# Summing two states per step on GpSimd or on TensorE: moving the switch from step 190 to step 224

## The chip, the cores and the metric

The kernel runs on one core of a Trainium2 chip. A core has five engines with a queue each: TensorE (PE in the profile; PEld is its weight load), VectorE (DVE), ScalarE (ACT), GpSimd (POOL) and SyncE (SP, which issues most of the DMAs). Each engine works through its own queue in order and waits at semaphores for the others. The metric is the device time of one execution in microseconds (us); several executions are timed, and the median is given. One further execution is profiled, and all views of the profile come from that one.

## The reference, cut to what matters

The input x has 2 sequences of 2048 tokens with 256 features. After a layer norm it goes two ways. One is a Mamba block followed by an MLP; the other is a mixture of 8 experts with the 2 best chosen per token. The result is x + s * silu(g), with s from the first way and g from the second. The core of the Mamba block, and the part that the change touches, is the recurrence over time with 512 channels and 16 states per channel:

```python
def step(h, ts):
    dt_t, B_t, C_t, u_t = ts
    dA = jnp.exp(dt_t[..., None] * A)
    h = h * dA + (dt_t * u_t)[..., None] * B_t[:, None, :]
    y = jnp.einsum('bds,bs->bd', h, C_t)
    return (h, y)
```

followed by `y = ys + xc * D`, `y = y * silu(z)`, the output projection, `x = x + ...` and `x = x + silu(rmsnorm(x) @ mlp_w1.T) @ mlp_w2.T`. The einsum sums h * C over the 16 states. Everything is computed in float32.

## The kernel before

**Tiling.** The 4096 tokens are cut into 8 blocks of 512 (`c`, 0 to 7; blocks 0 to 3 are the first sequence, 4 to 7 the second). The 512 channels are 4 groups of 128 partitions (`d`). The 16 states are taken in pairs (`g`, 0 to 7). A **step** `n` is one block, one channel group and one pair of states: `n = 32 c + 8 d + g`, 256 steps in all. Steps 190 and 191 are the last two of block 5, steps 192 to 223 are block 6, steps 224 to 255 are block 7.

**One step** runs over several engines:

- ACT computes the two decays `da` (`exps`, L1387), two steps ahead.
- DVE multiplies dt*u by the broadcast B of both states (L1498, into PSUM) and runs two scans along time, one per state (L1502), which give `h`.
- POOL saves the last column of `h` for the next block (`save`, L1424; not in blocks 3 and 7), multiplies `h` by the broadcast C (`times_c`, L1430, one instruction of 128x1024) and, if the step is *paired*, adds the two states into one (L1432, 128x512).
- PE adds the step to the sum over the states in PSUM by multiplying `h` with an identity matrix (`accumulate`, L1400): one product for a paired step, two for an unpaired one. It does so three steps later (`LAG = 3`). The first product of a group is the skip `xc * D` (L1396).

`h` has five buffers, so the scan of a step waits until PE has read the step five before it. The tiles B and C are loaded once per block for each `g` by SP (`load_bc`, L762), as soon as the old ones were read for the last time: B by DVE's L1498, C by POOL's L1430.

**Work between the steps.** The function `draw` lets other work in between by a budget of PE time per half step (`HALF = 1.93`): the projections of the next block (`front`: PE L621, ACT L631 to L638, DVE L646, ACT L660, PE L666, PE L685, then dt with POOL's L700, L712 and L713), the gate z (`gate_z`, PE L772), the output projection (`out_proj`, PE L821, DVE L855) and the FFN tiles: first 39 tiles of the experts, then the MLP in 16 half blocks of 256 tokens. `Later` puts off the instructions that follow on other engines by a number of half steps. The budget does not look at whether a step is paired, so the written order of the other instructions is independent of it.

**A half block of the MLP** takes: rows from DRAM, scaled on ACT (L1119), turned on PE (L934), first product on PE (L946), silu on ACT (L1144, with a table load, L183, before and after), second product on PE (L958). Beside it, POOL issues four gathers of the two experts' rows (L1185), ACT weighs them (L1199), POOL adds them (L1203), ACT takes a tanh (L1207), and DVE ends the half: L1218, L1228 (needs the tanh), L1229, L1230, then SP stores it. The rows are gathered into tiles that the half before has used, so the gathers follow its L1229. The PSUM tile of the second product shares its one bank with the output projection (L821), which therefore follows L1230. The first products, the turned rows and the projections share three banks, in order (`bank("h", ...)`).

Which steps are paired is said by one line:

```python
return n >= 8 and not (n >= 190 and n % 2 == 0) and n < NS - 1
```

Here `NS` is 256. Before step 8 no step is paired, from 8 to 189 every step, and from 190 on only the odd ones.

Of the kernel before, what the change touches and what calls it, by code (L numbers as in the profile page):

```python
# [52 lines left out]
def kernel(  # L53
# [1321 lines left out]
    NS = NBLK * ND * (DS // 2)  # L1375
# [15 lines left out]
    def accumulate(n):  # L1391
        c, d, g = at[n]
        if g == 0:
            y_n[c, d] = ring("y", 1)
            ys[c, d] = ps_1.tile([P, T], F32, tag="y", name=f"y{c}_{d}")
            nc.tensor.matmul(ys[c, d], ddiag[:, d, :], xcs[c, d], start=True, stop=False)  # L1396
            skips[0] += 1
        nq = 1 if paired(n) else 2
        for q in range(nq):
            nc.tensor.matmul(  # L1400
                ys[c, d], ident, hts[n][:, q, :], start=False,
                stop=(g == DS // 2 - 1 and q == nq - 1),
            )
        if g == DS // 2 - 1:
            y, sz, twice = ys[c, d], szs[c, d], 1.0 if d else 0.5

            def gated():
                nc.vector.scalar_tensor_tensor(sz, y, twice, sz, ALU.mult, ALU.mult)
                y_made.add((c, d))

            later.put(gated, y_n[c, d], after=2)
# [14 lines left out]
    def times_c(n):  # L1426
        c, d, g = at[n]

        engine = nc.vector if n == NS - 1 else nc.gpsimd
        engine.tensor_tensor(hts[n], hts[n], bct[c, "C", g], ALU.mult)  # L1430
        if paired(n):
            nc.gpsimd.tensor_tensor(hts[n][:, 0, :], hts[n][:, 0, :], hts[n][:, 1, :], ALU.add)  # L1432

    def paired(n):

        return n >= 8 and not (n >= 190 and n % 2 == 0) and n < NS - 1

    def draw(share):

# [146 lines left out]
```

## Time and profile before

| what | value |
|---|---|
| time, median of 3 runs | 1489.96 us (1489.83 to 1492.37) |
| profiled execution, its own time | 1505.4 us |
| its span (first to last instruction) | 1503.7 us |
| POOL L1430 (times C), per instruction | 2371 ns mean, 255 instructions |
| POOL L1432 (adds two states) | 1287 ns mean, 214 instructions |
| PE L1400 (identity product), trace records | 596; one product leaves two records |
| DVE L1502 (scan) | 1270 ns mean |
| start of L1430 for steps 190, 222, 224 | 1083.66, 1278.36, 1286.08 us |

The page gives times from one profiled execution, which took some 15 us longer than the median of the timed runs. In a group's row, after the count, stand the busy time in us and the mean of one in ns, then the engine's idle time before these instructions and what ended most of it. In a list of waits, `A <- B: 15.7, 5, 6.2` says that A sat idle for 15.7 us in all until B ended, 5 times, at longest 6.2. In a timeline a row has the start and the length in us, and in brackets the idle time before it. "issue" is a wait that the profile ties to nothing.

### The profile page before, as it was taken

Reading aid. Unit: us, or ns where it says so; the run is one execution under the profiler, and the core shown is the slowest. Engines: PE = TensorE matmul, PEld = TensorE weight load, DVE = VectorE, ACT = ScalarE, POOL = GpSimd, SP = SyncE. Lnnn points to the kernel's source line nnn. Section 1 sums busy time; section 2 is a strip of 40 time slices with the busy share of each in tenths; the row PEclk is TensorE's granted clock in tenths of the full one; section 3 lists DMA queues with packets and bytes.
Section 4 is the critical chain, followed back from the end, with each engine's and each line's share of the span. In section 5 each row is a group of like instructions: output and inputs, shape, how many; then the busy total and the mean of one; then the engine's idle time right before and its main releaser. Section 6 shows DMA issues by size and latency. Waiting matters only on the chain.

```text
span 1503.7 us, 18025 instructions
## 1 busy us (share of the span) xinstructions
PE 1347.4 (90%) x5122; PEld 944.1 (63%) x5122; DVE 1217.2 (81%) x1351; ACT 978.5 (65%) x1765; POOL 1188.3 (79%) x964
## 2 busy tenths in 40 slices
PE   5744799999999999999999999979878998999958
PEld 4531467765776677766776677546655666667726
DVE  7448888889798998799888988999767967888853
ACT  4742777458655776568656865677648988778932
POOL 2665779987898799968997899889975888777860
PEclk9556899999999999999999999999999999999989
DMA  5568134962477345924492449445830116412110
GB/s 187 198 234 304 46 99 145 306 220 76 125 230 280 92 131 180 335 95 121 158 363 74 129 140 331 167 139 175 268 114 8 55 53 211 139 53 60 57 57 14
DMA packets 169317, 231.85 MB, mean 154 GB/s; under 512 B 19825, under 2 KB 139761, under 8 KB 169217
## 3 DMA queue, kind: packets, MB, share of 16 engines
q1 hardware_dynamic: 163072, 213.91, 42.9%
q0 software_dynamic: 6144, 16.79, 3.4%
q8 instruction: 41, 0.67, 0.2%
q14 instruction: 60, 0.48, 0.1%
HBM read 195.12 MB, written 35.52 MB: 153 GB/s over the span
## 4 chain that ended last, share of the span: by engine, by line
PE 44%; POOL 25%; DVE 10%; ACT 10%; issue 6%; DMA 4%; another core or an unknown queue 1%; POOLq 0%; DVEq 0%; SPq 0%; ACTq 0%
POOL h L1430 13%; PE phe L946 9%; PE y L1400 8%; PE poe L958 8%; POOL h L1432 6%; PE pom L958 4%; PE phm L946 4%; PE po L821 3%; ACT L183 2%; PE px L621 2%; DVE h L1502 2%; DMA B<-bcd 2%; ACT da L1387 2%; PE pz L772 2%; DMA C<-bcd 1%
## 5 line engine op out<-in xcount | busy, mean ns | idle before, releaser
L1430 POOL TENSOR_TENSOR h<-h,C 128x1024 f32<-128x1024 f32 x255 | 604.1, 2371 | 36.7 <-issue 11.5
L1502 DVE TENSOR_TENSOR_SCAN h<-da,hs,b 128x512 f32<-128x512 f32 x384 | 477.6, 1270 | 41.4 <-PE y L1400 10.8
L1387 ACT ACTIVATE da<-dt,a_neg 128x512 f32<-128x512 f32 x512 | 352.8, 717 | 93.3 <-DVE h L1502 87.2
L1400 PE MATMUL y<-h,ident 128*128 128x512 f32 x596 | 307.3, 617 | 34.6 <-POOL h L1432 17.5
L1498 DVE TENSOR_TENSOR b<-du,B 128x1024 f32<-128x1024 f32 x256 | 315.0, 1231 | 18.4 <-DMA B<-bcd 9.1
L1432 POOL TENSOR_TENSOR h<-h 128x512 f32<-128x512 f32 x214 | 275.4, 1287 | 16.8
L946 PE MATMUL phe<-xsTe,w_e 128*128 128x256 f32 (+1 forms) x1248 | 268.1, 366 | 9.4 <-ACT xsTe L937 7.6
L946 PEld LDWEIGHTS phe<-xsTe,w_e 128*128 128x128 f32 x1248 | 225.4, 194 | 72.7 <-issue 27.6
L958 PE MATMUL poe<-w_e,hide 128*128 128x256 f32 x1136 | 265.2, 380 | 2.5 <-ACT hide L1053 2.5
L958 PEld LDWEIGHTS poe<-w_e,hide 128*128 128x128 f32 x1136 | 213.8, 190 | 65.1 <-issue 33.5
L1053 ACT ACTIVATE hide<-phe,b 128x256 f32<-128x256 f32 (+1 forms) x312 | 123.6, 450 | 140.8 <-PE phe L946 140.4
L1400 PEld LDWEIGHTS y<-h,ident 128*128 128x128 f32 x596 | 112.2, 197 | 124.0 <-issue 60.5
L1502 DVE TENSOR_TENSOR_SCAN h<-da,b 128x512 f32<-128x512 f32 x128 | 151.3, 1210 | 12.7 <-PE y L1400 4.8
L183 ACT ACT_TABLE_LOAD x121 | 155.2, 1283 | 2.9 <-PEq L1573 0.8
L946 PE MATMUL phm<-xsTm,w_m 128*128 128x256 f32 x512 | 121.0, 387 | 2.7 <-ACT hidm L1144 2.0
L1424 POOL COPY hs<-h 128x2 f32<-128x2 f32 x192 | 42.0, 219 | 100.9 <-DVE h L1502 89.4
L958 PE MATMUL pom<-w_m,hidm 128*128 128x256 f32 x512 | 121.0, 386 | 0.0
L946 PEld LDWEIGHTS phm<-xsTm,w_m 128*128 128x128 f32 x512 | 99.1, 194 | 29.6 <-issue 10.8
L958 PEld LDWEIGHTS pom<-w_m,hidm 128*128 128x128 f32 x512 | 98.5, 194 | 25.2 <-issue 12.5
L462 POOL DMA_INDIRECT xs_d<-xt,slot x64 | 64.0, 1000 | 49.1 <-issue 21.4
L646 DVE SCALAR_TENSOR_TENSOR xc<-px,par_sb,xc 128x512 f32<-128x512 f32 x96 | 71.6, 748 | 30.4 <-ACT xc L638 25.6
L1185 POOL DMA_INDIRECT yk<-ys_d,row_y x60 | 58.3, 972 | 22.6 <-issue 14.2
(221 smaller groups left out, 1366.7 us busy)
## 6 DMA issues: line engine op xcount, KB each, us to landing
w_e<-in_w SPq DMA_DIRECT2D x312, 256.0 KB
B<-bcd SPq DMA_DIRECT2D x64, 512.0 KB
C<-bcd SPq DMA_DIRECT2D x64, 512.0 KB
xs<-xs_d SPq DMA_DIRECT2D x32, 256.0 KB
ys_d<-ys SPq DMA_DIRECT2D x32, 256.0 KB
b<-in_b SPq DMA_DIRECT2D x39, 128.0 KB
xnr<-xnd SPq DMA_DIRECT2D x16, 256.0 KB
xom<-in_x SPq DMA_DIRECT2D x16, 256.0 KB
```

What stands on the lines that cost most here:

```text
L183: nc.scalar.preload_act_table_set(name)
L462: r = nc.gpsimd.indirect_dma_start(out=xs_d, out_offset=bass.IndirectOffsetOnAxis(ap=slot[:, k, i : i + 1], axis=0), in_=x_of(i // J, i % ...
L646: nc.vector.scalar_tensor_tensor(v[:, s : s + T], px, conv_w[:, d, KC - 1 - s : KC - s], v[:, s : s + T], ALU.mult, ALU.add,)
L946: nc.tensor.matmul(ph[:, q, :], self.w1[c0 // 2][:, k, ts(q, P)], self.xT[:, k, :], start=(k == 0), stop=(k == KM - 1),)
L958: nc.tensor.matmul(po[:, j, :], self.hid[c // 2][:, c % 2, ts(j, P)], self.w2[c // 2][:, c % 2, :], start=(c == 0 and j == 0), stop=(c == ...
L1053: nc.scalar.activation(hc[:, q, :], ph[:, q, :], AF.Relu, bias=self.b1[:, c0 + q : c0 + q + 1])
L1387: nc.scalar.activation(das[n][:, q, :], dts[c, d], AF.Exp, scale=a_neg[:, d, 2 * g + q : 2 * g + q + 1])
L1400: nc.tensor.matmul(ys[c, d], ident, hts[n][:, q, :], start=False, stop=(g == DS // 2 - 1 and q == nq - 1),)
L1430: engine.tensor_tensor(hts[n], hts[n], bct[c, "C", g], ALU.mult)
L1432: nc.gpsimd.tensor_tensor(hts[n][:, 0, :], hts[n][:, 0, :], hts[n][:, 1, :], ALU.add)
L1498: nc.vector.tensor_tensor(inp, dus[c, d].unsqueeze(1).to_broadcast([P, 2, T]), bct[c, "B", g], ALU.mult,)
L1502: nc.vector.tensor_tensor_scan(hts[n][:, q, :], das[n][:, q, :], inp[:, q, :], 0.0 if c % CPB == 0 else hs[c - 1][:, d, 2 * g + q : 2 * g ...
```

## The change

One number changes. The even steps 190, 192, ... 222, seventeen steps, become paired: POOL adds their two states with L1432, and PE reads one tile with L1400 instead of two. In block 7 the even steps stay unpaired. The order of all other instructions on the five engines is the same as before.

```diff
     def paired(n):
 
-        return n >= 8 and not (n >= 190 and n % 2 == 0) and n < NS - 1
+        return n >= 8 and not (n >= 224 and n % 2 == 0) and n < NS - 1
```

## The prediction

> **What bounds the kernel now.** I read the page's engine rows first, then the groups of the line that the change touches, then the waits in the stretch where it acts, and last the order of instructions at the waits that matter.
>
> ```profile
> span 1503.7 us, 18025 instructions
> PE 1347.4 (90%) x5122; PEld 944.1 (63%) x5122; DVE 1217.2 (81%) x1351; ACT 978.5 (65%) x1765; POOL 1188.3 (79%) x964
> L1430 POOL TENSOR_TENSOR h<-h,C 128x1024 f32<-128x1024 f32 x255 | 604.1, 2371 | 36.7 <-issue 11.5
> L1400 PE MATMUL y<-h,ident 128*128 128x512 f32 x596 | 307.3, 617 | 34.6 <-POOL h L1432 17.5
> L1432 POOL TENSOR_TENSOR h<-h 128x512 f32<-128x512 f32 x214 | 275.4, 1287 | 16.8
> ```
>
> PE looks like the bound and POOL (GpSimd) has room, which would favour the change at once. But these are means over the whole run. Counting L1430 on POOL's timeline, step 190 is at 1083.66 and step 222 at 1278.36. In 1083.66 to 1286.08 the busy times are PE 181.6, DVE 157.2, ACT 161.9 and POOL 160.0 of 202.4 us: nobody is full, so the waits must tell who is late. Of this stretch (up to 1320) the list of waits says:
>
> ```profile
> ACT yk L1207 <- POOL yk L1203: 15.7, 5, 6.2
> ...
> DVE pom L1228 <- ACT yk L1207: 10.7, 4, 4.2
> ...
> PE po L821 <- DVE xom L1230: 9.4, 2, 6.1
> ```
>
> Read it from the top down. Each half block of the MLP needs a sum on POOL (L1203), then a tanh on ACT (L1207), then a product on DVE (L1228) that stands in DVE's queue ahead of the scans, and twice the next product of PE (L821) waits for DVE's last step. ACT waits for POOL's L1203 in five of the seven halves. So at these points POOL is the late engine, though it is 79% busy. The timelines show one such point (columns: start, length, engine, line; in brackets the idle time before it and what ended it):
>
> ```profile
> 1095.17 2.37 POOL L1430 TENSOR_TENSOR h<-h,C 128x1024 f32<-128x1024 f32 x1
> 1097.47 0.19 POOL L1424 COPY hs<-h 128x2 f32<-128x2 f32 x1
> 1097.75 2.37 POOL L1430 TENSOR_TENSOR h<-h,C 128x1024 f32<-128x1024 f32 x1
> 1100.19 1.26 POOL L1432 TENSOR_TENSOR h<-h 128x512 f32<-128x512 f32 x1
> 1101.41 1.26 POOL L1203 TENSOR_TENSOR yk<-yk,yk 128x512 f32<-128x512 f32 x1
> ...
> 1102.71 0.63 ACT L1207 ACTIVATE yk<-yk 128x512 f32<-128x512 f32 x1 [3.66 <-POOL yk L1203]
> ...
> 1103.37 0.70 DVE L1228 SCALAR_TENSOR_TENSOR pom<-yk,pom 128x512 f32<-128x512 f32 x1 [2.46 <-ACT yk L1207]
> ...
> 1105.74 5.79 PE L821 MATMUL po<-ow_sb,sz 128*128 128x256 f32 x16 [6.15 <-DVE xom L1230]
> ```
>
> POOL runs here without a wait, and every engine after it in the chain is idle until it is done.
>
> **The change, part by part.** It affects the 17 even steps 190 to 222; the order on every engine stays as it was.
>
> *Added on POOL:* one L1432 per such step. Without it the copy after L1430 comes 1097.47 - 1095.17 = 2.30 us after L1430 began; with it, L1203 comes 1101.41 - 1097.75 = 3.66 us after. So 1.36 us each, 17 x 1.36 = 23.1 us.
>
> *Removed on PE:* one 128x512 product per such step, two of the trace's records. The four records of an unpaired step take 1087.45 to 1089.17 = 1.72 us, the two of a paired step 0.86 (1078.40 to 1079.26). So 0.86 us each, 17 x 0.86 = 14.6 us.
>
> *Moved:* nothing, but the sum of an even step is ready 1.36 us later for PE, which asks for it three steps later.
>
> What counts is where each piece lies. I follow the lateness against the profile of before through five stretches.
>
> Stretch 1, 1083.66 to 1105.74. The adds of 190 and 192 come before the L1203 at 1101.41, POOL has no wait between, and the three engines behind are idle: 2 x 1.36 = **+2.7** at PE's L821. PE's savings of 190 are lost, since PE then waits 1.80 us for POOL's add of step 191 at 1095.02 anyway.
>
> Stretch 2, to 1165.7. Here POOL is the early one. It waits 1.61, 5.14, 1.27, 1.22, 6.58, 4.33 and 1.82 us before its copies, for DVE's scans mostly, so the five adds of 194 to 202 (6.8 us) cost nothing. If that cover were gone they would be +6.8. PE is on the path from 1112 to 1128, and sheds the products of 192 and 194: -1.7, leaving **+1.0**. From 1129 the path is ACT, with DVE's convolution behind it, so the savings of 196 to 202 only lengthen PE's waits.
>
> Stretch 3, to 1216.6. The adds of 204 and 206 vanish in two waits of POOL for ACT, 1.80 us at 1182.96 and 1.58 at 1191.16. Those of 208 and 210 lie in an unbroken run of POOL up to the L1203 at 1215.32, for which ACT idles 6.17 us and DVE 3.56: +2.7, together **+3.7**.
>
> Stretch 4, to 1286.1. ACT works without a pause from 1216.6 to 1261, so PE's savings change nothing. The adds of 212, 214, 216 and 218 (5.4 us), less POOL's waits of 0.37 and 1.89, delay the L1203 at 1263.90 by 3.7 + 3.2 = 6.9; ACT waits for it already (3.72). The adds of 220 and 222 (2.7), less 1.2 of the 1.27 us that POOL waits at 1269.00 before its gathers and the 0.2 before L1203, make the L1203 at 1284.84 late by **+8.2**; ACT had waited 0.16 for it.
>
> Stretch 5, to 1313.15, where POOL comes out of a wait of 6.00 us and nothing is added any more. Of the 8.2, the gathers' wait of 0.62 and 1.7 us of slack between tanh (ended 1305.5) and DVE's L1228 (1307.17) give back 2.3: +5.9. From there all engines are late by the same amount to the end.
>
> Two rules bear on this. The row first: after 3.92 us of idle PE, the four records of L621 at 1144.03 took 3.68 us instead of 1.88, and after the 6.15 us above, L821 took 5.79 instead of 3.72; the row of those 5 us (columns: from and to, length, busy time and instructions of PE, PEld, DVE, ACT and POOL, then the granted clock, DMA share, GB/s) shows the clock at 0.50:
>
> ```profile
> 1105.00:1110.00 5.00, 4.26 (x10) 3.48 (x11) 1.78 (x2) 1.33 (x2) 3.23 (x4) 0.50 0.15 52
> ```
>
> The Trainium skill, page "TensorE: Matmul & The Clock Gate", section "What's actually happening", says that an idle window of about 3.4 us takes the array to half speed and about as much busy time is needed to come back. This speaks against the change: less work and later partners make PE's gaps longer. In stretch 5 PE, by then only 1.4 us late, would wait for ACT to free a bank before the L946 of 1291.07 (ACT's L1144 at 1288.10 is 8.2 late), some 4.5 us: a new cold start, +1.8 by the row of 3.92 us, on the way to the product that DVE needs at 1306.37. Without the rule the sum is +5.9, with it +7.7. I take **+7.0**: the gap lies close to the threshold and the window's place is not known.
>
> The other rule would make the adds dearer: the page "SBUF — State Buffer", section "Who interferes with whom", says that a DVE instruction with two SBUF inputs and a GpSimd instruction that reads SBUF shut each other out. Of DVE's work in the stretch only L1495 is such in number; the scans and L1498 take one input from PSUM. It has 4 instructions with 3.15 us together, against 0.67 undisturbed: 0.5 us lost in all. By the rule at worst each waits for one more add, 4 x 1.27 = 5.1; by the row nothing changes, as POOL was already busy there. I take 0 and keep 5.1 for the upper end.
>
> *Queues:* the sync engine loads block 7's C tiles after L1430 of steps 216 to 223, and other loads stand behind those. At most 8 us late; the first (issued 1248.55) is needed at 1286.08, and the MLP rows behind them (1265.76, 1285.15) at 1274.59 and 1296.08, which move along by 4 us or more. Cost 0; if landing took all that slack, about +2.
>
> **The sum.** Profiled execution: 1503.7 of span and 1.7 around it, 1505.4, goes to about 1512.4. The median runs, 1489.96, are 15 us quicker than the profiled one without my knowing where; the delay is carried over unchanged: **1497.0 us**, +0.5%.
>
> **Rivals.**
>
> *PE decides, and the kernel is faster.* PE is 90% busy, and on the chain that ended last I find the products of the changed steps 192, 194, 198, 200, 216, 218, 220 and 222: 8 x 0.86 = 6.9, so 1483. It takes over if ACT's tanh really was not held by POOL (a releaser is inferred), that is, if less than 0.5 of the 1.36 us of each add passes through. Against it: eight of these adds lie where POOL has no wait.
>
> *All hidden.* POOL idles 42 us in the stretch, more than 23.1. An all-paired stage, steps 184 to 191, took 1034.24 to 1081.89 = 47.7 us with POOL 95% busy, no longer than the four of block 6 (50.6, 48.1, 46.3, 49.5). Then 1490, within 3 us. Against it: the later stages hold two gathers and two L1203 each; the fourth has 43.3 us of POOL work, with four adds and the gaps between gathers 50.5 of 49.5.
>
> *POOL becomes the bound throughout:* all adds pass except the five of stretch 2: 12 x 1.36 = 16.3 plus a cold start, 1507.
>
> **How the numbers follow.** The forecast has 0.60, with its own range of 1493 to 1502 (+3 where more waits absorb, +12 with the port's 5.1). Faster by PE 0.13, hidden 0.12, POOL throughout 0.15. Runs of this kernel tell about 0.2%, 3 us, from no change: faster 0.13, same 0.12, slower 0.75. The range goes to 1487 below, where it takes in the hidden case and leaves out the faster one, and to 1506 above, where it leaves out half of the last rival.
>
> **What would show it.** L1432 x231 at about 1.29 us and L1400 x562. The wait of L1207 for L1203 longer than 15.7 us in this stretch. The distance from the L1430 of step 190 to that of step 224 at 209 to 211 us instead of 202.4, no lateness gained in steps 196 to 202, and from step 227 on the same times as before. I am wrong if L1207's wait does not grow, if the distance shrinks (PE), or if steps 196 to 202 too get longer (POOL throughout).

## The result and the profile after

The changed kernel takes 1501.69 us (median of 5 runs, 1499.76 to 1504.22); beside it the kernel before took 1492.04 us (5 runs, 1489.83 to 1493.59). The ratio is 1.007 with an interval of 1.0059 to 1.0081: **slower by 9.65 us** by the medians (10.4 by the ratio). The forecast was +7.0 us (1489.96 to 1497.0). In the experiments below, the us beside a ratio come from the ratio and the median of before on the same chip; where the difference of the medians parts from them by more than 0.5 us, it is given too. One execution of the first experiment took 7185.84 us and enters no figure.

The page of the changed kernel, the rows that answer to those of before:

```profile
span 1502.4 us, 17964 instructions
PE 1334.7 (89%) x5088; PEld 935.4 (62%) x5088; DVE 1217.6 (81%) x1351; ACT 978.4 (65%) x1765; POOL 1210.2 (81%) x981
L1400 PE MATMUL y<-h,ident 128*128 128x512 f32 x562 | 294.7, 622 | 42.6 <-POOL h L1432 23.7
L1432 POOL TENSOR_TENSOR h<-h 128x512 f32<-128x512 f32 x231 | 296.6, 1284 | 18.1
```

What was moved is what was said: 17 more adds at 1284 ns, 34 fewer records of products. PE got 12.7 us less busy and POOL 21.9 us more, and nobody is full. But the span, 1502.4 us, is *shorter* than the 1503.7 us of before, although the timed runs are longer. One profiled execution cannot be held against another by its end. In before, the L1495 of step 184, which no changed instruction precedes, starts at 1034.24; in after it starts at 1023.72:

```profile
1023.72 2.53 DVE L1495 TENSOR_TENSOR du<-dt,xc 128x512 f32<-128x512 f32 x1
```

So the profiled execution of after had run ahead by 10.52 us before the change could act. All lateness below is counted from this instruction: the start in the kernel at hand, plus its own shift (10.52 us here), less the start in before. Read so, the trace gives +9.37 us over the whole of block 7, near the +9.65 us of the timed runs.

| place (start in before) | forecast | after |
|---|---|---|
| L821 of block 5, 1105.74 | +2.7 | +2.80 |
| L666 of block 7, 1171.95 | +1.0 | +1.01 |
| L1203, 1215.32 | +3.7 | **+5.39** |
| L1203, 1263.90 | +6.9 | +8.61 |
| L1203, 1284.84 | +8.2 | +9.92 |
| L821 of block 6, and all later | +7.0 | +9.37 |

The list of waits of after, for the same stretch (1073 to 1310; wait in us in all, times, longest):

```profile
ACT yk L1207 <- POOL yk L1203: 27.8, 5, 8.8
DVE pom L1228 <- ACT yk L1207: 22.6, 5, 5.8
...
PE phm L946 <- ACT hidm L1144: 11.8, 4, 3.3
...
PE po L821 <- DVE xom L1230: 10.7, 2, 7.5
```

ACT's wait for POOL's sum grew from 15.7 to 27.8 us, and DVE's wait for the tanh behind it from 10.7 to 22.6. The timelines of POOL, PE and ACT show the first of these places, and the two where the lateness later changed (start, length, engine, line; in brackets the idle time before it and what ended it):

```profile
1090.05 2.34 POOL L1430 TENSOR_TENSOR h<-h,C 128x1024 f32<-128x1024 f32 x1
1092.47 1.26 POOL L1432 TENSOR_TENSOR h<-h 128x512 f32<-128x512 f32 x1
1093.69 1.26 POOL L1203 TENSOR_TENSOR yk<-yk,yk 128x512 f32<-128x512 f32 x1
...
1098.02 5.53 PE L821 MATMUL po<-ow_sb,sz 128*128 128x256 f32 x16 [7.47 <-DVE xom L1230]
...
1162.44 5.30 PE L666 MATMUL pxd<-xc,xp_sb 128*48 128x512 f32 x8 [2.45 <-DVE xc L646]
...
1211.49 0.63 ACT L1207 ACTIVATE yk<-yk 128x512 f32<-128x512 f32 x1 [8.84 <-POOL yk L1203]
```

The first four lines are the forecast's mechanism: POOL runs on without a gap, the add lies ahead of L1203, and PE's wait before L821 grows from 6.15 to 7.47 us, by one add; the work that PE does before this wait was 1.5 us late already, by the other add. The L666 line is what the forecast did not have.

### The profile page after: what moved, and what is told of

Same layout as the page of the kernel before. It is cut to its first block, busy times and chain, and to the rows that moved or that the text cites. A ratio compares the mean times of both kernels' runs of the same rounds, so it can differ in the third digit from the quotient of the medians.

```text
span 1502.4 us, 17964 instructions
## 1 busy us (share of the span) xinstructions
PE 1334.7 (89%) x5088; PEld 935.4 (62%) x5088; DVE 1217.6 (81%) x1351; ACT 978.4 (65%) x1765; POOL 1210.2 (81%) x981
## 5 line engine op out<-in xcount | busy, mean ns | idle before, releaser
L1400 PE MATMUL y<-h,ident 128*128 128x512 f32 x562 | 294.7, 622 | 42.6 <-POOL h L1432 23.7
L1432 POOL TENSOR_TENSOR h<-h 128x512 f32<-128x512 f32 x231 | 296.6, 1284 | 18.1
L946 PE MATMUL phe<-xsTe,w_e 128*128 128x256 f32 (+1 forms) x1248 | 267.4, 365 | 10.1 <-ACT xsTe L937 7.3
L946 PEld LDWEIGHTS phe<-xsTe,w_e 128*128 128x128 f32 x1248 | 224.3, 193 | 74.1 <-issue 28.4
L1400 PEld LDWEIGHTS y<-h,ident 128*128 128x128 f32 x562 | 106.2, 198 | 125.2 <-issue 52.0
L1502 DVE TENSOR_TENSOR_SCAN h<-da,b 128x512 f32<-128x512 f32 x128 | 151.3, 1211 | 12.7 <-PE y L1400 4.8
L946 PE MATMUL phm<-xsTm,w_m 128*128 128x256 f32 x512 | 122.9, 392 | 12.4 <-ACT hidm L1144 11.8
L946 PEld LDWEIGHTS phm<-xsTm,w_m 128*128 128x128 f32 x512 | 100.0, 196 | 41.2 <-ACT hidm L1144 15.2
L821 PE MATMUL po<-ow_sb,sz 128*128 128x256 f32 x256 | 60.8, 392 | 17.7 <-DVE xom L1230 11.9
```

The lines of the kernel that those rows point to most:

```text
L946: nc.tensor.matmul(ph[:, q, :], self.w1[c0 // 2][:, k, ts(q, P)], self.xT[:, k, :], start=(k == 0), stop=(k == KM - 1),)
L1400: nc.tensor.matmul(ys[c, d], ident, hts[n][:, q, :], start=False, stop=(g == DS // 2 - 1 and q == nq - 1),)
L1502: nc.vector.tensor_tensor_scan(hts[n][:, q, :], das[n][:, q, :], inp[:, q, :], 0.0 if c % CPB == 0 else hs[c - 1][:, d, 2 * g + q : 2 * g ...
```

## The experiments

Eleven kernels ran, each beside runs of the kernel before on its chip. "Lateness" is always taken from the trace as above; two traces agree to some 0.3 us in it where nothing differs. "Cold" is said of an instruction group on PE that ran in part at a granted clock of 0.50, "warm" of one at 1.00.

### One half of the steps each

Only the seven steps 194 to 206, which the forecast held to be covered:

```diff
-        return n >= 8 and not (n >= 190 and n % 2 == 0) and n < NS - 1
+        return n >= 8 and not (n >= 190 and n % 2 == 0 and not 194 <= n <= 206) and n < NS - 1
```

> Only the seven even steps 194 to 206 are newly paired, those whose adds the prediction called hidden. The prediction's chain (lateness comes only through L1203): no lateness from the adds; TensorE sheds two products on the path (-1.7), a cold start at L666 may give 1.7 back: -1.7 to +1.5 us against before. GpSimd's load as such (every one of the 17 adds costs the same): 7/17 of 9.65 = +4.0.

Only the other ten, 190, 192 and 208 to 222:

```diff
-        return n >= 8 and not (n >= 190 and n % 2 == 0) and n < NS - 1
+        return n >= 8 and not (n >= 190 and n % 2 == 0 and (n >= 224 or 194 <= n <= 206)) and n < NS - 1
```

> The complement: only the ten even steps 190, 192 and 208 to 222 are newly paired. The chain: nearly the whole delay, +2.7 from the first two and +4 to +7 from the rest, +7 to +10 us. Load as such: 10/17 of 9.65 = +5.7.

Measured: the seven 1.0018 [1.0004, 1.0033], +2.7 us (0.9 by the medians), the trace +0.1; the ten 1.0077 [1.0049, 1.0104], +11.6 us (8.8 by the medians; one of the four runs took 1521.24), the trace +8.6. So the place of an add decides and not the number of adds: seven of seventeen cost near nothing and ten carry the delay. By the ratios both lie above what the chain let expect (+1.5 and +10 at most), by the medians and the traces inside it. The interval of the seven, 0.6 to 5.0 us, also takes in the +4.0 of the load as such; it is the trace that speaks against that. The ten are +7.1 late up to the L821 of block 6, which was cold (5.38 us for 3.69) and added 1.7.

The two kernels differ in one more thing. L666 of the seven and of the ten, from PE's timelines:

```profile
1171.43 5.30 PE L666 MATMUL pxd<-xc,xp_sb 128*48 128x512 f32 x8 [2.68 <-DVE xc L646]
```

```profile
1172.65 3.60 PE L666 MATMUL pxd<-xc,xp_sb 128*48 128x512 f32 x8 [0.55 <-ACT xc L660]
```

With the products of 194 to 202 gone, PE idles 2.68 us before L666 and then needs 5.30 us for it; with them kept it idles 0.55 us, as before, and needs 3.60.

### Adds alone, products alone

The two halves of the edit, each without the other: the adds by the new rule and PE's products by the old one (the second state is then counted twice), and the reverse (the second state of those steps is left out of the sum). Both with a second rule that only the number of products follows:

```diff
-        nq = 1 if paired(n) else 2
+        nq = 1 if one_product(n) else 2
```

> GpSimd's 17 adds alone: TensorE still reads both tiles, so that for these steps the second state is counted twice. The chain: the adds are the cause, so +8 to +11 us; without the shed products stretch 2 gives nothing back (+1.7), but TensorE has no longer gaps before L666 (-1.7). If the loss is TensorE's cold starts in the gaps left by the products that were taken away: +5 or less.

> The 17 products taken from TensorE without the adds: the second state of these steps is left out of y. The chain: TensorE is not the late engine at most of them, so -2.5 to +1.5 us. The first rival of the prediction (TensorE decides): -6.9. If cold starts from longer gaps are the loss: +3 or more.

Measured: adds alone 1.0076 [1.0057, 1.0095], +11.4 us, the trace +9.9. Products alone 0.9991 [0.9984, 0.9998], -1.35 us, the trace -1.9. So all 17 products that PE no longer makes, 14.6 us of its work, are worth 1.35 us; PE is not the engine that is late at most of them, busy as it is. A part of their worth was lost again: the trace is 3.4 us early at the L821 of block 6, and that came out cold after a longer wait:

```profile
1304.95 5.38 PE L821 MATMUL po<-ow_sb,sz 128*128 128x256 f32 x16 [3.76 <-DVE xom L1230]
```

The adds alone have the same at this place (+8.4 before it). Their +11.4 us (12.3 by the medians) are above the upper end that was expected (+11) by the timed runs and inside it by the trace. In neither is L666 slowed (PE's wait before it is 0.55 and 1.83 us): its long wait needs both parts, PE's products gone and POOL's adds of the same steps, which the seven have too.

### Where L666's cold start goes

Both readings can now be put side by side, by the tanh (L1207) that before has at 1148 and at 1216.62:

| kernel | L666 | at 1148 | at 1217 | gained |
|---|---|---|---|---|
| the ten (adds of 208, 210 on the way) | 3.60 us | +1.61 | +4.27 | 2.66 |
| adds alone (204 to 210) | 3.60 us | +2.99 | +5.61 | 2.62 |
| after with 200, 202 put back (below) | 3.60 us | +1.51 | +4.16 | 2.65 |
| the seven (204, 206 only) | 5.30 us | -0.67 | +1.00 | 1.67 |
| after (204 to 210) | 5.30 us | +1.04 | +5.38 | 4.34 |
| after with eight products more (last below) | 5.30 us | +0.96 | +5.29 | 4.33 |

Two terms explain all six rows: 2.7 us for the adds of 208 and 210, as forecast, and 1.7 us wherever L666 takes 1.7 us longer (5.30 - 3.60). The adds of 204 and 206 give nothing where L666 is warm, as forecast.

To try this by itself, two steps of the changed kernel were put back, so that PE has their products again and no long gap before L666:

```diff
-        return n >= 8 and not (n >= 224 and n % 2 == 0) and n < NS - 1
+        return n >= 8 and not (n >= 224 and n % 2 == 0 or n in (200, 202)) and n < NS - 1
```

> The changed kernel with steps 200 and 202 unpaired again. If TensorE's cold start at L666 (5.30 us in the changed kernel, 3.60 before) comes from the gap that these two shed products leave: L666 takes 3.6 us again, its wait falls from 2.45 to 1 us or less, and the delay falls by 1.7 to about +7.9 us over before. If it doesn't come from them, or doesn't matter: +9 to +10.

Measured: 1.005 [1.0034, 1.0067], +7.5 us, near the +7.9 expected. In PE's timeline:

```profile
1160.90 3.60 PE L666 MATMUL pxd<-xc,xp_sb 128*48 128x512 f32 x8 [0.38 <-DVE xc L646]
...
1305.16 5.38 PE L821 MATMUL po<-ow_sb,sz 128*128 128x256 f32 x16 [3.21 <-DVE xom L1230]
```

L666 is warm again and the tanh at 1217 is 1.2 us less late. But the trace ends at +9.7, no better than after, because in this execution L821 of block 6 came out cold after a wait of 3.21 us (5.38 us; in after 3.69 after the same wait). So the part at L666 is shown, while the total of 7.5 us (8.2 by the medians) has an interval (5.1 to 10.0) that also takes in the 9.65 of after.

### The chain taken away

If the delay goes through POOL's L1203, then a sum made on DVE must take it away. The same edit in after and in before:

```diff
-                nc.gpsimd.tensor_tensor(yk[0], yk[0], yk[1], ALU.add)
+                nc.vector.tensor_tensor(yk[0], yk[0], yk[1], ALU.add)
```

> The changed kernel with L1203, the sum that the tanh waits for, on VectorE instead of GpSimd in all 16 half blocks. The chain (lateness reaches the others through L1203): the waits of L1207 for L1203 in this stretch, 27.8 us in the changed kernel, go to nearly nothing, and the kernel lies within +4 us of the kernel before. Load as such: GpSimd loses 7 sums of 1.27 in the stretch but keeps 17 adds, so +9.65 less some 5: about +5, with other waits for GpSimd in place of these.

> The kernel before with L1203 on VectorE, the partner of the run on the changed kernel. The chain: the 15.7 us of waits of L1207 for L1203 in this stretch go, and the kernel gets faster by 3 to 8 us; the change made on top of it then costs less than half of 9.65. Load as such: also faster, by about 5, but the change on top still costs 9 to 10.

Measured: after with it 1500.91 us, before with it 1500.54 us, beside 1493.59 us for before itself: 1.0047 [1.0031, 1.0064] and 1.0045 [1.0029, 1.0062]. Two things follow. **The change then costs 0.4 us by the medians instead of 9.65** (each of the two ratios has an interval of 2.5 us to either side); in the traces the L1228 at 1307 is +3.2 in the one and +1.4 in the other, 1.8 apart instead of 9.4, and 2.7 in the last half blocks. ACT's wait for L1203 falls from 27.8 to 2.0 us. So the adds are harmful because they stand ahead of L1203 in POOL's queue; that DVE, now late itself, hides a part of their cost is not excluded. After with it is 7 us over before, more than either reading had let expect (+4 and +5). And the second: before did not gain the 3 to 8 us that were expected of it, but lost 6.7. The waits of after, and then of before, with the sum on DVE:

```profile
DVE yk L1203 <- ACT yk L1199: 23.3, 6, 6.4
```

```profile
DVE yk L1203 <- ACT yk L1199: 19.6, 7, 5.5
...
PE po L821 <- DVE xom L1230: 13.4, 2, 8.5
```

In before with the sum on DVE, DVE stands in its queue until ACT has weighed the gathered rows (L1199), 19.6 us in all, and the scans stand behind it. The wait was moved to an engine with more behind it, and PE waits 13.4 us before L821 where it waited 9.4.

### The change turned round

By the same reading the kernel before should gain if POOL got less work ahead of its late sums. Six odd steps there are unpaired:

```diff
-        return n >= 8 and not (n >= 190 and n % 2 == 0) and n < NS - 1
+        return n >= 8 and not (n >= 190 and n % 2 == 0 or n in (191, 193, 209, 211, 217, 219)) and n < NS - 1
```

> The change turned round where GpSimd is late: of the kernel before, the odd steps 191, 193, 209, 211, 217 and 219 are unpaired as well, so GpSimd does six adds less ahead of three of the sums that the tanh waits for. The chain: 2.7 us each in the first two places and 0 to 2 in the third, where ScalarE and TensorE are about as late: -4 to -7 us. If TensorE decides: +5 (six products of 0.86).

Measured: 0.9997 [0.9988, 1.0006], no gain; expected were 4 to 7 us. The trace shows that it was made and lost again: L1203 is 2.6 us early at 1101, 3.5 at 1215, 5.8 at 1264, ACT's wait for it falls to 6.8 us, and still at 1307 L1228 is 2.2 us early. The gain went in two steps. Between 1264 and 1285 it fell from 5.8 to 3.1 us: ACT waits for PE's L946, and PE, which has more products to make, works there without a gap. ACT's waits at these two places were 0.01 and 1.81 us in before:

```profile
1249.94 0.60 ACT L1144 ACTIVATE hidm<-phm 128x512 f32<-128x512 f32 x1 [1.66 <-PE phm L946]
1253.38 0.60 ACT L1144 ACTIVATE hidm<-phm 128x512 f32<-128x512 f32 x1 [2.85 <-PE phm L946]
```

Then came L821 of block 6, from PE's timeline, and the row of 5 us inside it (busy time of PE, PEld, DVE, ACT, POOL, then the granted clock):

```profile
1293.63 6.73 PE L821 MATMUL po<-ow_sb,sz 128*128 128x256 f32 x16 [3.21 <-DVE xom L1230]
...
1295.00:1300.00 5.00, 5.00 (x14) 3.89 (x13) 2.11 (x2) 0.72 (x1) 2.68 (x2) 0.52 0.21 63
```

L821 took 6.73 us instead of 3.69, and block 7 runs 0.6 us *late*.

To see what the cold L821 is worth, products on an identity matrix that nobody reads were put ahead of L821 of blocks 5 and 6 (five and three of 128x512), so that PE does not idle there: in the kernel above, in before, and in after.

```diff
+                if hf == 0 and c in (5, 6):
+                    idle = 5 if c == 5 else 3
+                    warm, n_warm = bank("h", [P, T], f"warm{c}")
+                    for k in range(idle):
+                        nc.tensor.matmul(
+                            warm, ident, xrT[c + 1][:, 0, :], start=(k == 0), stop=(k == idle - 1),
+                        )
+                    drop(*n_warm)
                 po, n = bank("o", [P, JS, DM], f"po{c}_{hf}")
```

> The kernel with the six odd steps unpaired, with five products (block 5) and three (block 6) into a bank that nobody reads, placed on TensorE in its two waits before L821. There GpSimd's six adds less had made it 2 to 3 us early up to step 226, and a cold start of L821 (6.73 us instead of 3.69 after the same wait of 3.21) took that away. If the cold start is what took it: L821 takes 3.5 to 3.8 us both times, and the kernel is 3 to 6 us faster than before. If something else holds the time at that place: no change, -1 to +1.

> The kernel before with the same eight products and nothing else. L821 of block 5 (5.79 us after a wait of 6.15) takes 3.7: -1 to -3 us if the clock is the cause, in block 6 nothing to gain (3.69). If the products only cost time: +0 to +3.

> The changed kernel with the same eight products. L821 of block 5 took 5.53 us: -1 to -2 against the changed kernel, so +7 to +9 over before, since the waits for GpSimd are untouched. If the products only cost time: +9.6 or more.

Measured: 0.9987 [0.9972, 1.0002] (trace -2.9), 0.999 [0.9977, 1.0003] (trace -3.3) and 1.0055 [1.0038, 1.0072] (trace +9.2). L821 in the three, in this order (of block 6, then of block 5 twice):

```profile
1312.94 3.69 PE L821 MATMUL po<-ow_sb,sz 128*128 128x256 f32 x16 [0.64 <-DVE xom L1238]
```

```profile
1106.64 3.69 PE L821 MATMUL po<-ow_sb,sz 128*128 128x256 f32 x16 [1.85 <-DVE xom L1238]
```

```profile
1106.86 5.35 PE L821 MATMUL po<-ow_sb,sz 128*128 128x256 f32 x16 [3.19 <-DVE xom L1238]
```

(L1238 is the L1230 of the other kernels, moved by the eight lines above it.) In the first two L821 is warm; before alone takes 2.1 us less for the L821 of block 5 (3.69 for 5.79), and the trace gives just these 2.1 back at 1137. So L821's cold start is on the path. But it is not what kept the turned-round kernel from gaining: with both L821 warm, that kernel (-2.9 in the trace, 1503.60 us) is no better than before with the same products (-3.3, 1503.61 us), and the 3 to 6 us that were expected of it did not come. At 1264 it is 7.4 us early against 2.2, at 1285 3.8 against 3.3: what POOL saves, PE's additional products take back there. In after the five products were done too early: 3.19 us of wait were left and L821 stayed cold, so this run doesn't tell what after would be without that start, and its +8.3 us lie in the expected +7 to +9 without the reason that was given for them. The timed gains, 2.0 and 1.5 us by the ratios, have intervals that take in 1: no version was shown to beat the kernel before.

## Why the prediction was right, and what was mis-sized

**Slower, through POOL's L1203: right.** Products alone, adds alone and the sum on DVE each show it. That PE decides (1483 us) is refuted by the products alone (-1.35 us for 14.6 us of PE's work). That all is hidden is refuted by the +9.65 us. That POOL is the bound throughout is refuted by the seven covered steps in the trace (+0.1 us); their timed runs (+0.9 by the medians, +2.7 by the ratio) leave some doubt about the size, not about the place, as the ten others alone give +8.8 or more.

**Step by step.** An add costs 1.36 us where POOL runs without a wait: two of them ahead of the first L1203 gave +2.80 for +2.7. Stretch 2 gave the +1.01 of the forecast: the five adds of 194 to 202 vanished in POOL's waits for DVE, and PE's two products were won. Stretch 4 gave 4.53 for 4.5. The way of step 190 to step 224 took 212.19 us, a little more than the 209 to 211 of the forecast, and no lateness was gained in steps 196 to 202.

**The mis-sized term is stretch 3**, +3.7 at 1215.32, which measured +5.39: a slower L666 was put at nothing. The sentence that failed is "the savings of 196 to 202 only lengthen PE's waits": they did, from 0.55 to 2.45 us before L666, and this longer wait was not free. The forecast gave the path to ACT from 1129 on, but the chain that ended last in before goes through L666, between ACT's L660 and its copy L671:

```profile
1171.96 3.61 PE pxd L666 x8
```

In after the granted clock fell to 0.50 for 3.41 us inside L666 (its first 0.76 us ran at 1.00), where before had 1.00 at the same place (1170 to 1175). Half of 3.41 us is the 1.7 us that L666 took longer:

```profile
1159.79:1163.20 3.41, 0.96 (x3) 0.29 (x3) 3.34 (x5) 2.76 (x6) 3.03 (x3) 1.00 0.27 78
1163.20:1166.61 3.41, 3.41 (x5) 0.81 (x4) 3.27 (x4) 2.80 (x4) 3.25 (x4) 0.50 0.00 0
```

L666 feeds ACT's copy (L671) and the work up to L699, and this feeds POOL's dt work, so ACT came 1.7 us later too, and POOL's waits for it, in which the adds of 204 and 206 were to vanish, moved along: they were still there (0.76 us at 1175.16, 1.61 at 1183.36, for 1.80 and 1.58), but behind them everything was later. The forecast had weighed the rule of the cold start at one gap, the one before L946, and not at those that the edit's own savings lengthen.

**Stretch 5** gave back 0.55 instead of 1.2. The new gap came where it was said, before L946, and was shorter than said, 2.75 us for 4.5, since PE itself was 4.7 us late by then and not 1.4; the cold start came all the same (PE's timeline of after):

```profile
1288.13 2.49 PE L946 MATMUL phm<-xsTm,w_m 128*128 128x256 f32 x8 [2.75 <-ACT hidm L1144]
1290.41 1.91 PE L1400 MATMUL y<-h,ident 128*128 128x512 f32 x2
1292.12 2.28 PE L946 MATMUL phm<-xsTm,w_m 128*128 128x256 f32 x8
```

These took 1.89, 1.02 and 1.89 us in before: 1.9 us more, against 1.8 forecast with the cold start. That this cold start was on the path, the ten show, which had the same wait at the same place and stayed warm:

```profile
1296.59 1.99 PE L946 MATMUL phm<-xsTm,w_m 128*128 128x256 f32 x8 [2.75 <-ACT hidm L1144]
```

There the lateness fell from +8.8 at L1203 to +7.1 at L1228, by the 1.7 us of slack that the forecast had seen behind the tanh; the 0.6 us of the gathers' wait came back in neither. The forecast had gone between a sum without the rule (+5.9) and one with it (+7.7); it took the middle. The two terms, 1.7 and 0.65 us, make the difference between +7.0 and the +9.37 of the trace; what the timed runs have beyond that, 0.3 us, is inside their interval. The sign and the path were reasoned out; how near the number came is in part luck, as the traces went cold at different places: after at L666 and L946, the ten and the adds alone at the L821 of block 6.

**The port.** The five L1495 from 1081.89 to 1276.35 took 7.26 us in all, for 4.80 in before, so the price that was set to 0 exists: 2.5 us, half of the bound of 5.1. None of it is seen in the lateness: over the L1495 of 1221.74 (1.78 us for 0.67) that at ACT's tanh goes from +5.38 to +5.40.

## What to carry to other kernels

Look for the wait that ends last and follow its queue backwards. The same add cost 1.36 us in an unbroken run ahead of an awaited sum and nothing where its engine was waiting for another, and 14.6 us of work taken off the busiest engine were worth 1.35 us, since that engine was not the late one at most places. Which engine is late changes with the place and with the edit: six adds less on POOL gained 5.8 us, and the products that PE got for them took back 2.7 of these within 21 us. Work taken off an engine that isn't late comes back as longer gaps: price each gap that the edit lengthens, not only the new ones, where a pause makes the work after it slower.

## What the runs showed of the hardware

**How long a pause slows TensorE depends on more than its length.** Before L666, waits of 0.38 to 1.83 us were followed by 3.60 us, and waits of 2.13, 2.45, 2.54 and 2.68 us by 5.30. Before the L821 of block 6, the same wait of 3.21 us was followed by 3.69 us (before, after), by 5.38 (after with two steps put back) and by 6.73 (before with six steps unpaired). The Trainium skill, page "TensorE: Matmul & The Clock Gate", section "What's actually happening", has an idle window of about 3.4 us, which is free-running, so that the moment of the change varies with the work's place in it. The traces agree with the window, and show that it need not be idle. In each of the 13, the granted clock changes only on a grid of 3.41 us, and the grid lies differently against the work in each. Between 900 and 1430 us there are 103 such windows at full clock in which PE was busy for less than 42% of the time: after each of them the clock was 0.50. After 1735 windows with PE busy for over half, it was 0.50 five times; why is open. From 0.50 it went back to 1.00 after a window with PE busy for 84% or more, and only then. The same wait of 3.21 us lies across two windows in before, each over half busy, and for the most part in one window in after with two steps put back (rows as above, one per window, before first):

```profile
1304.55:1307.96 3.41, 1.78 (x9) 1.22 (x7) 1.40 (x2) 1.85 (x3) 2.61 (x2) 1.00 0.00 0
1307.96:1311.38 3.42, 1.84 (x9) 1.66 (x10) 3.34 (x4) 0.00 (x0) 0.00 (x0) 1.00 0.32 87
1311.38:1314.79 3.41, 3.41 (x14) 2.25 (x13) 3.16 (x4) 1.48 (x4) 1.64 (x1) 1.00 0.22 69
```

```profile
1302.31:1305.72 3.41, 0.56 (x3) 0.54 (x4) 3.17 (x5) 0.56 (x1) 0.98 (x1) 1.00 0.00 0
1305.72:1309.13 3.41, 3.41 (x10) 2.70 (x9) 2.88 (x3) 0.46 (x1) 0.36 (x1) 0.50 0.58 154
```

So a pause of 2 to 3 us cost half a window, 1.7 us, or nothing, as the grid fell, and 3.0 us before the L821 of 6.73, where PE was busy for 80% of the first window at 0.50 and the next was at 0.50 too. A cold start in the profiled execution need not be in the timed ones; how many of those had L666 cold, no run here shows.

**The level differs between groups of runs, and for the most part before the change acts.** The kernel before took 1492.04 and 1493.59 us in two groups of runs (the later groups were each made on one chip) and 1505.1 and 1505.41 in two others. The traces of the group at 1493.59 reach the L1495 of step 184 by 10.9 to 13.7 us sooner than the profiled execution of before (1505.4 us); those of the group at 1505.1 lie within 2.8 us of it, those of the group at 1505.41 from 1.8 us sooner to 6.3 us later. The before with six steps unpaired is only 0.6 us late at the end of its trace, and its profiled execution took 1493.66 us, having reached step 184 13.7 us sooner. So most of the 15 us that the forecast could not place lie before step 184, and adding the delay unchanged to the median was right. What makes the start slower was not tried.

**VectorE's sum beside a busy GpSimd.** L1203 took 1.27 us on POOL each time; on DVE it took 0.67 to 2.42 us, 1.34 in the median, in after and 0.69 to 2.72 us, 1.24 in the median, in before, so even its own time was hardly a gain.
